# First attention: the next batch's normalization in four parts, its matmul pieces two a step, the rotary tables one part a step

## The chip, the core and the metric

The kernel runs on one core of one Trainium2 chip. The time is the device time of one launch in microseconds (us). Five instruction queues work side by side: TensorE (PE in the profile, its weight loads PEld), VectorE (DVE), ScalarE (ACT), GpSimd (POOL) and SyncE (SP), which here issues the DMAs. Each executes its own instructions in order; semaphores tie them together.

## The reference

All arrays are 32-bit floats; x is 8 batches of 512 tokens of 256 numbers. Four residual blocks follow each other:

```
x = x + attn_a(layernorm(x))     # 8 heads of 64, keys and values from a 64-wide latent
x = x + ffn(layernorm(x))        # 2 layers: local attention with rotary tables, then a gated MLP
x = x + attn_b(layernorm(x))     # 16 heads of 16, causal
x = x + ffn(layernorm(x))
```

What the change touches is the first block:

```
h = (x - mean(x)) / sqrt(var(x) + 1e-5)
q = h @ Wq.T ; lat = h @ Wkv_down.T
scores = q @ (lat @ Wk_up.T).T / 8 ; attn = softmax(scores)
x = x + concat(attn @ (lat @ Wv_up.T)) @ Wo.T
```

It also touches the preparation of the rotary tables, which the local attention of the second block multiplies its queries and keys with. These are cos and sin tables, scaled by position, times the learned query and key scales: two layers by four tables of 512 x 64 numbers.

## The kernel before

The eight batches go in two groups of four. Each group runs ten stages: the first attention (`attention_a`), two times local attention and feedforward, the second attention (`attention_b`), and again two times local attention and feedforward. A stage is a `head()`, whose parts the stage ahead calls one by one in its last steps, and a `run()`.

**Steps of the first attention.** A tile is 128 tokens. A unit is one pair of heads for one tile of queries (4 x 4 units a batch). Units go two at a time: `steps()` has 32 pairs in a group, so 8 steps a batch, numbered m = 0 to 31 (and two more to drain). In step m the scores of pair m are made, the probabilities of pair m-1 are transposed, and the values of pair m-2 are multiplied. On TensorE a step is: scores (4 matmuls, L393), values (16, L439), the transposes of one unit (8, L426), the transposes of the other unit, and in an odd step from m = 3 on the projection of a finished tile (4, L455). On VectorE: two maxima (L399), per unit the copy of its transposes out of PSUM (L430) and a reciprocal of its sums (L414), and in an odd step the add of the projection to x (L458). On ACT: in an odd step the copy of the values (oT, L449), then four exponentials (L244), then four divisions (L419). Everything issued in a step is tied, engine by engine, to the order in which the code writes it (`order_keeper`).

**Pieces.** The following batch's `prologue` is a generator that the steps advance: a piece in the middle of an odd step and one at the end of an even step. Its pieces are, in order: the layernorm (four times `bn_stats` and `bn_aggr` on VectorE, L279 and L280; two POOL operations for 1/sqrt, L269 and L270; four normalizing operations on VectorE, L286), two halves of the transposed yT (4 transposes each, copied by ACT, L352), pd (2 matmuls, copied to latT by VectorE, L359), pl (4 transposes, copied by ACT, L365) and four times pq (2 matmuls, copied to a part of qT by ACT, L376). The layernorm stands at the end of a batch's step 0, the last pq at the end of the next batch's step 0.

**Buffers.** PSUM: three buffers "s" of two banks, which scores and transposes take in turn (four a step); one bank "mm", which all pieces and the projection share; one bank "o" for the values. In SBUF the probabilities have three buffers "p".

**Tables.** `rotation_tables()` is called once, after the head of the first stage, in which step 0 of the first group is already issued. It loads the raw tables into a buffer "p", the scales into a buffer "two", and issues eight multiplications on VectorE (L230), outside the kept order. What is outside a kept order is placed by a scheduler when the program is built; so are the first parts of the next stage (for example the statistics `st_f0x` of the local attention), which stand where the scheduler puts them, between the instructions of a step.

**The second group's head.** Its parts are called two by two in the six rounds of the last feedforward batch of the group before, and two more times ahead of that batch's output matmuls. By then step 0 is issued.

Of the kernel before, what the change touches and what calls it, by code (L numbers as in the profile page):

```python
# [11 lines left out]
F32 = mybir.dt.float32  # L12
AF = mybir.ActivationFunctionType
ALU = mybir.AluOpType
# [3 lines left out]
P = 128  # L18
NB, T, D = 8, 512, 256
NT = T // P  # L20
GROUP = 4
H, HD = 8, 64
# [8 lines left out]
DEPTH = 2  # L31
EARLY_STEPS = 2
LN_EPS = 1e-5
# [16 lines left out]
def kernel(  # L50
# [26 lines left out]
    nc = tc.nc  # L77
# [5 lines left out]
    def load_x(b):  # L83
        xt = resid.tile([P, NT, D], F32, tag=f"x{b % GROUP}", name=f"x_{b}")
        nc.sync.dma_start(xt, x[b].rearrange("(t p) d -> p t d", p=P))
        return xt
# [7 lines left out]
    pool = ctx.enter_context(tc.tile_pool(name="work", bufs=2))  # L94
# [8 lines left out]
    xs = {0: load_x(0)}  # L103
# [115 lines left out]

    def rotation_tables():  # L220

        raw = pool.tile([P, 4, NT, HD], F32, tag="p", name="raw", bufs=3)
        nc.sync.dma_start(raw, rope.rearrange("c (t p) d -> p c t d", p=P))
        sc = pool.tile([P, DEPTH, 4, HD], F32, tag="two", name="sc", bufs=5)
        nc.sync.dma_start(
            sc.rearrange("p l c d -> p (l c d)"), f_scale.rearrange("l c d -> (l c d)").partition_broadcast(P)
        )
        for l in range(DEPTH):
            for c in range(4):
                nc.vector.tensor_mul(tabs[l][:, c], raw[:, c], sc[:, l, c].unsqueeze(1).to_broadcast([P, NT, HD]))  # L230

    tabs = [const.tile([P, 4, NT, HD], F32, name=f"tab{l}") for l in range(DEPTH)]

    phase = {"start": None, "last": [], "gates": False}
# [31 lines left out]
    def inv_sqrt(t, least, op, n, name):  # L266

        r = pool.tile([P, n], F32, tag=f"rs{n}", name=name, bufs=3)
        nc.gpsimd.tensor_scalar(r, t, least, 1.0, op, ALU.mult)  # L269
        nc.gpsimd.tensor_tensor(r, r, neg_half[:, :n], ALU.pow)  # L270
        return r

    def row_statistics(halves, name):

        st = pool.tile([P, NT, len(halves), 6], F32, tag=f"ln_st{len(halves)}", name=f"st_{name}", bufs=2)
        mv = pool.tile([P, NT, 2], F32, tag="ln_mv", name=f"mv_{name}", bufs=2)
        for t in range(NT):
            for i, h in enumerate(halves):
                nc.vector.bn_stats(st[:, t, i, :], h[:, t, :])  # L279
            nc.vector.bn_aggr(mv[:, t, :], st[:, t].rearrange("p i s -> p (i s)"))  # L280
        return mv, inv_sqrt(mv[:, :, 1], LN_EPS, ALU.add, NT, f"rstd_{name}")

    def normalize_rows(halves, dst, mv, rstd):
        for t in range(NT):
            for h, d in zip(halves, dst):
                nc.vector.tensor_scalar(  # L286
                    d[:, t, :], h[:, t, :], mv[:, t, 0:1], rstd[:, t : t + 1], ALU.subtract, ALU.mult
                )

    def layernorm(halves, dst, name):  # L290

        normalize_rows(halves, dst, *row_statistics(halves, name))

    def transposed(ps, rows, half, name):

        pt = ps.tile([P, NT, P], F32, tag="mm", name=name)
        for t in range(NT):
            nc.tensor.transpose(pt[:, t, :], rows[half][:, t, :], ident)
        return pt.rearrange("p t c -> p (t c)")

    def halves_of(rows):
        return [rows[:, :, 0:P], rows[:, :, P:D]]
# [7 lines left out]
    def attention_a(batches, g):  # L310
# [33 lines left out]
        def prologue(b):  # L344

            n = f"a{b}"
            yr = pool.tile([P, NT, D], F32, tag="yr", name=f"yr_{n}", bufs=1)
            layernorm([xs[b]], [yr], n)
            yield
            yT = pool.tile([P, 2, T], F32, tag="hT", name=f"yT_{n}")  # L350
            for k in range(2):
                nc.scalar.copy(yT[:, k, :], transposed(ps_mm, halves_of(yr), k, f"pyt_{n}_{k}"))  # L352
                yield

            pd = ps_mm.tile([P, T], F32, tag="mm", name=f"pd_{n}")
            for k in range(2):
                nc.tensor.matmul(pd, lhsT=wd_a[:, k, :], rhs=yT[:, k, :], start=(k == 0), stop=(k == 1))
            latT = pool.tile([P, T], F32, tag="two", name=f"latT_{n}", bufs=5)
            nc.vector.tensor_copy(latT, pd)  # L359
            yield  # L360
            pl = ps_mm.tile([P, NT, HD], F32, tag="mm", name=f"pl_{n}")
            for t in range(NT):
                nc.tensor.transpose(pl[:, t, :], latT[:HD, t * P : (t + 1) * P], ident[:HD, :HD])
            lat = pool.tile([P, NT, HD], F32, tag="lat", name=f"lat_{n}")
            nc.scalar.copy(lat, pl)  # L365
            yield
            qT = big([P, 4, T], f"qT_{n}")
            if b == batches[0]:
                fold()
            for m in range(4):  # L370
                pq = ps_mm.tile([P, T], F32, tag="mm", name=f"pq_{n}_{m}")
                for k in range(2):
                    nc.tensor.matmul(
                        pq, lhsT=wqk_a[:, k, m * P : (m + 1) * P], rhs=yT[:, k, :], start=(k == 0), stop=(k == 1)
                    )
                nc.scalar.copy(qT[:, m, :], pq)  # L376
                state[b] = qT, latT, lat
                yield
# [87 lines left out]
        each = NT * 2  # L466

        def steps(ahead):
            tables_of(EXP_TABLES)
            kept_order = order_keeper()  # L470
            pieces = iter(())

            def pair(m):
                return pairs[m] if 0 <= m < len(pairs) else ()

            for m in range(len(pairs) + 2):
                new, turning, weighted = pair(m), pair(m - 1), pair(m - 2)
                done = weighted[1] if weighted and m % 2 else None
                with kept_order():
                    for some in new:  # L480
                        some.scores()
                    for some in weighted:
                        some.values()
                    for some in new:
                        some.maxima()
                    if done:
                        done.keep_values()
                    for some in new:
                        some.exponentials()
                    if turning:  # L490
                        turning[0].turn()
                        turning[0].keep_turned()
                    if new:
                        new[0].invert()
                    if done:
                        next(pieces, None)
                    if new:
                        new[0].divide()
                    if turning:
                        turning[1].turn()  # L500
                        turning[1].keep_turned()
                    if new:
                        new[1].invert()
                        new[1].divide()
                    if done:
                        done.project()
                        done.add()
                    else:
                        next(pieces, None)
                    if m % each == 0 and m // each + 1 < len(batches):  # L510
                        pieces = prologue(batches[m // each + 1])
                        next(pieces)
                if m > len(pairs) - 3:
                    ahead[0]()
                    ahead[0]()
                yield

        follower = []
        rest = steps(follower)

        def head():
# [14 lines left out]
    def attention_f(batches, l, g, ys, first_layer):  # L536
# [287 lines left out]
        stats = {}  # L824
# [6 lines left out]
        def rows(at):  # L831
            b, t = tiles[at]
            if first_layer and t == 0:
                ys[b] = rows_space(b, f"y_{g}_{b}")
                normalize_rows([xs[b]], [ys[b]], *stats.pop(b))

        def begin(at):
            if tiles[at][1] == 0:
# [94 lines left out]
    def feedforward(batches, l, g, ys, last, finish, norms):  # L933
        w1, w2 = weights_g(l, g)

        h2s, stats, hns, hTs, made = {}, {}, {}, {}, {}
# [11 lines left out]
        def halves(b):  # L948
            return [ys[b][:, :, 0:P], h2s[b]]
# [4 lines left out]
        def rows(b):  # L954
            hn = pool.tile([P, 2, NT, P], F32, tag="yr", name=f"hn_g{g}_{b}", bufs=1)
            hns[b] = [hn[:, 0], hn[:, 1]]
            normalize_rows(halves(b), hns[b], *stats.pop(b))

        def columns(b, k):
            if k == 0:  # L960
# [135 lines left out]
    def normalized_b():  # L1096

        state, got = {}, {}

        def statistics(b):  # L1100
            got[b] = row_statistics([xs[b]], f"b{b}")

        def rows(b):
            yr = rows_space(b, f"yr_b{b}")
            normalize_rows([xs[b]], [yr], *got.pop(b))
            state[b] = {"yr": yr}

        return (statistics, rows), state
# [542 lines left out]
```

## Time and profile before

| | us |
|---|---|
| three runs | 4433.58, 4436.53, 4437.04 (median 4436.53) |
| the profiled execution | 4432.33 |
| its span, first to last instruction | 4430.5 |
| first attention, group 0, step 0 to step 31 | 27.2 to 293 |
| first attention, group 1, step 0 to step 31 | 2226.7 to 2489 |

The time of each step of the first attention is the distance between the starts of two steps' first score matmuls in the timeline (us):

| batch | 0 | 1 | 2 | 3 | 4 | 5 | 6 | 7 | sum |
|---|---|---|---|---|---|---|---|---|---|
| group 0, batch 0 | 6.90 | 14.17 | 6.22 | 9.34 | 6.23 | 9.66 | 7.43 | 9.66 | 69.61 |
| group 0, batch 1 | 7.43 | 11.32 | 6.22 | 9.34 | 6.23 | 9.66 | 7.43 | 9.66 | 67.29 |
| group 0, batch 2 | 7.43 | 13.68 | 6.22 | 9.34 | 6.22 | 9.66 | 7.43 | 9.66 | 69.64 |
| group 0, batch 3 | 7.43 | 9.79 | 6.23 | 8.67 | 6.22 | 8.67 | 6.22 | | |
| group 1, batch 0 | 12.01 | 5.40 | 6.23 | 9.33 | 6.23 | 9.66 | 7.43 | 9.66 | 65.94 |
| group 1, batch 1 | 7.43 | 11.33 | 6.22 | 9.34 | 6.22 | 9.66 | 7.43 | 9.66 | 67.30 |
| group 1, batch 2 | 7.43 | 13.18 | 6.22 | 9.33 | 6.23 | 9.66 | 7.43 | 9.66 | 69.14 |
| group 1, batch 3 | 7.43 | 9.79 | 6.22 | 8.67 | 6.22 | 8.67 | 6.22 | | |

In batch 3 there is no following batch, so from its step 1 on no pieces. Step 0 of group 1, batch 0, holds the output matmuls of the feedforward ahead. In the profile's rows, a bracket says how long the engine sat idle before the instruction and what ended that. Names are without buffer numbers: `s_a` scores, `nm_a` maxima, `p_a` probabilities, `ppt_a` and `pt_a` transposed probabilities in PSUM and SBUF, `o_a` values, `pp_a` projection, `rstd_a` the 1/sqrt of a normalization, `yr_a` its result; `f0x` and `f1x` are the local attention that follows in group 0 and 1. A matmul of these 32-bit numbers shows as two records.

### The profile page before, as it was taken

How to read it: one execution, taken by the hardware profiler on the slowest of the kernel's cores; microseconds unless marked ns; L12 is line 12 of the kernel's file. 1: busy time of each engine (PE TensorE's matmuls, PEld its weight loads, DVE VectorE, ACT ScalarE, POOL GpSimd, SP SyncE). 2: the span in 40 equal slices, each digit the busy share in tenths (PEclk: the TensorE clock that was granted, in tenths of full speed). 3: DMA queues.
4: the chain of work that ended last, by engine and by line, in shares of the span. 5: the costliest groups of instructions: out<-in, count | busy, mean ns of one | idle time of the engine just before them, and what ended most of it. 6: DMA issues, size and time to landing. Idle time of an engine off the chain costs nothing.

```text
span 4430.5 us, 70536 instructions
## 1 busy us (share of the span) xinstructions
PE 4175.9 (94%) x26580; PEld 2547.3 (57%) x26580; DVE 3073.0 (69%) x7497; ACT 2690.1 (61%) x6316; POOL 1147.7 (26%) x1140
## 2 busy tenths in 40 slices
PE   8999999999998899999999999999999988999999
PEld 5656556654555465566566565565545554655655
DVE  5668737846999887377466686377379998863773
ACT  5767616716989675177166675276178986742761
POOL 0014313311222342143100242143122223422431
PEclk9999999999999999999999999999999999999999
DMA  2000000000000000000100000000000000000000
GB/s 82 1 22 4 21 6 23 4 24 20 1 1 1 20 4 7 3 23 13 53 30 1 20 4 23 22 3 22 6 21 2 1 1 20 4 6 22 3 4 23
DMA packets 51091, 63.36 MB, mean 14 GB/s; under 512 B 6336, under 2 KB 45504, under 8 KB 50752
## 3 DMA queue, kind: packets, MB, share of 16 engines
q1 hardware_dynamic: 50752, 58.85, 4.1%
q8 instruction: 211, 3.46, 0.3%
q14 instruction: 128, 1.05, 0.1%
HBM read 46.28 MB, written 4.19 MB: 11 GB/s over the span
## 4 chain that ended last, share of the span: by engine, by line
PE 72%; DVE 14%; ACT 12%; issue 1%; POOL 1%; DMA 0%; SPq 0%; POOLq 0%; ACTq 0%; DVEq 0%
PE pu_g1x L983 3%; PE pu_g0x L983 3%; PE pu_g0y L983 3%; PE pu_g1y L983 3%; PE o_a L439 3%; PE s_a L393 3%; PE pqk_f0y L561 2%; PE pqk_f1y L561 2%; PE pqk_f0x L561 2%; PE pqk_f1x L561 2%; ACT r_b L244 2%; PE ppt_a L426 2%; PE ppt_b L1320 2%; DVE pt_b L1325 2%; ACT num_b L244 2%; DVE r_b L1271 2%
## 5 line engine op out<-in xcount | busy, mean ns | idle before, releaser
L1320 PE MATMUL ppt_b<-ident,num_b 128*128 128x128 f32 x1280 | 223.3, 291 | 89.5 <-DVE pt_b L1325 64.3
L1320 PEld LDWEIGHTS ppt_b<-ident,num_b 128*128 128x128 f32 x1280 | 137.4, 143 | 274.0 <-ACT num_b L244 96.7
L244 ACT ACTIVATE num_b<-num_b,most_b 128x512 f32<-128x512 f32 (+3 forms) x512 | 280.7, 552 | 20.2 <-POOL most_b L1300 19.8
L1325 DVE COPY pt_b<-ppt_b 128x512 f32<-128x512 f32 (+1 forms) x352 | 223.7, 635 | 31.7 <-PE ppt_b L1320 30.9
L244 ACT ACTIVATE p_a<-s_a,nm_a 128x512 f32<-128x512 f32 x256 | 173.3, 688 | 102.3 <-DVE nm_a L399 70.4
L430 DVE COPY pt_a<-ppt_a 128x1024 f32<-128x1024 f32 x128 | 155.7, 1219 | 106.3 <-PE ppt_a L426 106.3
L1267 DVE TENSOR_TENSOR t_b<-den_b,r_b 128x1024 f32<-128x1024 f32 (+1 forms) x176 | 197.1, 1120 | 45.5 <-ACT r_b L244 45.0
L1290 DVE CUSTOM_DVE_ANT_0 num_b<-num_b,r_b 128x512 f32<-128x512 f32 (+3 forms) x512 | 223.6, 485 | 1.2 <-POOL num_b L1283 1.2
L1283 POOL TENSOR_TENSOR num_b<-num_b,causal 128x256 f32<-128x256 f32 (+2 forms) x176 | 173.7, 987 | 184.1 <-ACT num_b L1277 183.6
L1248 PE MATMUL den_b<-st_b,st_b 18*128 18x384 f32 (+3 forms) x1024 | 208.0, 472 | 0.4 <-ACT num_b L1277 0.4
L1271 DVE SCALAR_TENSOR_TENSOR r_b<-t_b,r_b 128x1024 f32<-128x1024 f32 (+1 forms) x176 | 204.5, 1162 | 0.2
L1248 PE MATMUL dot_b<-st_b,st_b 16*128 16x384 f32 (+3 forms) x1024 | 189.5, 471 | 5.8 <-ACT yT_b L1126 4.4
L244 ACT ACTIVATE p_f0y<-p_f0y,nm_f0y,rn_f0y 128x256 f32<-128x256 f32 (+1 forms) x256 | 143.8, 563 | 80.6 <-DVE nm_f0y L700 80.5
L244 ACT ACTIVATE p_f1y<-p_f1y,nm_f1y,rn_f1y 128x256 f32<-128x256 f32 (+1 forms) x256 | 143.8, 564 | 80.6 <-DVE nm_f1y L700 80.5
L244 ACT ACTIVATE p_f1x<-p_f1x,nm_f1x,rn_f1x 128x256 f32<-128x256 f32 (+1 forms) x256 | 143.8, 564 | 76.8 <-DVE nm_f1x L700 76.7
L244 ACT ACTIVATE p_f0x<-p_f0x,nm_f0x,rn_f0x 128x256 f32<-128x256 f32 (+1 forms) x256 | 143.7, 563 | 76.8 <-DVE nm_f0x L700 76.8
L244 ACT ACTIVATE r_b<-den_b 128x1024 f32<-128x1024 f32 (+1 forms) x176 | 165.8, 942 | 36.6 <-PE dot_b L1248 17.7
L1300 POOL TENSOR_SCALAR most_b<-most_b 128x2 f32<-128x2 f32 (+2 forms) x176 | 34.2, 194 | 568.7 <-DVE most_b L1290 553.4
L1277 ACT ACTIVATE num_b<-dot_b 128x1024 f32<-128x1024 f32 (+1 forms) x176 | 164.6, 935 | 27.7 <-PE dot_b L1248 27.6
L399 DVE TENSOR_REDUCE nm_a<-s_a 128x2 f32<-128x1024 f32 x128 | 151.0, 1219 | 37.1 <-PE s_a L393 37.1
L244 ACT ACTIVATE r_b<-r_b 128x1024 f32<-128x1024 f32 (+1 forms) x176 | 172.5, 980 | 5.6
L603 POOL TENSOR_TENSOR ro_f1x<-ro_f1x,rs_f1x 128x512 f32<-128x512 f32 x64 | 80.4, 1278 | 363.0 <-DVE rs_f1x L592 149.7
(356 smaller groups left out, 11279.7 us busy)
## 6 DMA issues: line engine op xcount, KB each, us to landing
x<-in_x SPq DMA_DIRECT2D x8, 512.0 KB
out<-x SPq DMA_DIRECT2D x8, 512.0 KB
wf_0x<-in_f_wqkv SPq DMA_DIRECT2D x2, 1536.0 KB
wf_0y<-in_f_wqkv SPq DMA_DIRECT2D x2, 1536.0 KB
wf_1x<-in_f_wqkv SPq DMA_DIRECT2D x2, 1536.0 KB
wf_1y<-in_f_wqkv SPq DMA_DIRECT2D x2, 1536.0 KB
wg_0x<-in_f_w SPq DMA_DIRECT2D x2, 1386.0 KB
wg_0y<-in_f_w SPq DMA_DIRECT2D x2, 1386.0 KB
```

The source lines that it names most:

```text
L244: i = nc.scalar.activation(out, in_, func, **more).ins
L430: nc.vector.tensor_copy(got["pt"], got.pop("ppt"))
L561: nc.tensor.matmul(dst.rearrange("p h d -> p (h d)"), lhsT=hTs[b][:, k, t * P : (t + 1) * P], rhs=wqkv[:, k, c * INNER : (c + 1) * INNER], ...
L983: nc.tensor.matmul(pu[: cols.stop - cols.start, c], lhsT=w1[:, k, cols], rhs=hT[:, k, :], start=(k == 0), stop=(k == 1),)
L1248: return nc.tensor.matmul(s[:, a, m * width : (m + 1) * width], lhsT=left[at, j, past:width], rhs=right[at, j, :width], start=True, stop=True,
L1267: nc.vector.tensor_mul(t[:, :, :cols], den[:, :, :cols], r[:, :, :cols])
L1271: nc.vector.scalar_tensor_tensor(r[:, :, :cols], t[:, :, :cols], 2.0, r[:, :, :cols], ALU.subtract, ALU.mult)
L1277: nc.scalar.activation(num[:, :, :cols], dot[:, :, :cols], AF.Square, scale=-0.5)
L1283: nc.gpsimd.tensor_add(own, own, mask)
L1290: nc.vector.tensor_tensor_reduce(out=s4[:, a, m, :], in0=s4[:, a, m, :], in1=r4[:, a, m, :], scale=-1.0, scalar=LOWEST, op0=ALU.mult, op1= ...
L1320: nc.tensor.transpose(ppt[:, k, :], p[:, a, k * P : (k + 1) * P], ident)
L1325: nc.vector.tensor_copy(pt[:, a, :nblocks, :], ppt[:, :nblocks, :])
```

## The change

- The layernorm piece becomes four pieces: statistics of two tiles, statistics of the other two and the POOL operations, normalization of two tiles, normalization of the other two. The twelve pieces of a batch are advanced once at the end of every step, and once more in the middle of steps 4 to 7. So steps 0 to 3 carry one part of the normalization each, and steps 4 to 7 two pieces with matmuls each, the second after the projection and its add. No piece is left for the next batch's step 0.
- The raw tables go to the buffers "rs" and "ro", which only the local attention uses, and the eight multiplications are issued one a step in steps 4 to 11 of the first group, in kept order after the piece.
- The second group's head has three calls more and so fills all twelve calls of the six rounds.
- `row_statistics` and `normalize_rows` take a range of tiles and return or take one value more; their other callers do what they did.

```diff
     def rotation_tables():
-        raw = pool.tile([P, 4, NT, HD], F32, tag="p", name="raw", bufs=3)
+        raw = pool.tile([P, 4, NT, HD], F32, tag="rs", name="raw", bufs=1)
         nc.sync.dma_start(raw, rope.rearrange("c (t p) d -> p c t d", p=P))
-        sc = pool.tile([P, DEPTH, 4, HD], F32, tag="two", name="sc", bufs=5)
+        sc = pool.tile([P, DEPTH, 4, HD], F32, tag="ro", name="sc", bufs=3)
...
-        for l in range(DEPTH):
-            for c in range(4):
-                nc.vector.tensor_mul(tabs[l][:, c], raw[:, c], sc[:, l, c].unsqueeze(1).to_broadcast([P, NT, HD]))
+        def table(l, c):
+            nc.vector.tensor_mul(tabs[l][:, c], raw[:, c], sc[:, l, c].unsqueeze(1).to_broadcast([P, NT, HD]))
+        later.extend(lambda l=l, c=c: table(l, c) for l in range(DEPTH) for c in range(4))
...
-    def row_statistics(halves, name):
+    def row_statistics(halves, name, tokens=range(NT), made=None):
-        st = pool.tile([P, NT, len(halves), 6], F32, tag=f"ln_st{len(halves)}", name=f"st_{name}", bufs=2)
-        mv = pool.tile([P, NT, 2], F32, tag="ln_mv", name=f"mv_{name}", bufs=2)
-        for t in range(NT):
+        if made:
+            st, mv, _ = made
+        else:
+            st = pool.tile([P, NT, len(halves), 6], F32, tag=f"ln_st{len(halves)}", name=f"st_{name}", bufs=2)
+            mv = pool.tile([P, NT, 2], F32, tag="ln_mv", name=f"mv_{name}", bufs=2)
+        for t in tokens:
...
-        return mv, inv_sqrt(mv[:, :, 1], LN_EPS, ALU.add, NT, f"rstd_{name}")
+        rstd = inv_sqrt(mv[:, :, 1], LN_EPS, ALU.add, NT, f"rstd_{name}") if tokens[-1] == NT - 1 else None
+        return st, mv, rstd
...
         def prologue(b):
             n = f"a{b}"
+            some = None
+            for tokens in (range(2), range(2, NT)):
+                some = row_statistics([xs[b]], n, tokens, some)
+                yield
             yr = pool.tile([P, NT, D], F32, tag="yr", name=f"yr_{n}", bufs=1)
-            layernorm([xs[b]], [yr], n)
-            yield
+            for tokens in (range(2), range(2, NT)):
+                normalize_rows([xs[b]], [yr], *some[1:], tokens)
+                yield
...
-                    if done:
+                    if m % each > 3:
                         next(pieces, None)
...
                     if done:
                         done.project()
                         done.add()
-                    else:
-                        next(pieces, None)
                     if m % each == 0 and m // each + 1 < len(batches):
                         pieces = prologue(batches[m // each + 1])
-                        next(pieces)
+                    next(pieces, None)
+                    if later and m > 3:
+                        later.popleft()()
```

More of the change, by code (lines that the diff above doesn't have):

```diff
@@ L227, in rotation_tables @@
         )
-        for l in range(DEPTH):
-            for c in range(4):
-                nc.vector.tensor_mul(tabs[l][:, c], raw[:, c], sc[:, l, c].unsqueeze(1).to_broadcast([P, NT, HD]))
+        def table(l, c):
+            nc.vector.tensor_mul(tabs[l][:, c], raw[:, c], sc[:, l, c].unsqueeze(1).to_broadcast([P, NT, HD]))
+        later.extend(lambda l=l, c=c: table(l, c) for l in range(DEPTH) for c in range(4))
+    later = deque()
     tabs = [const.tile([P, 4, NT, HD], F32, name=f"tab{l}") for l in range(DEPTH)]
@@ L280, in row_statistics, with normalize_rows @@
             nc.vector.bn_aggr(mv[:, t, :], st[:, t].rearrange("p i s -> p (i s)"))
-        return mv, inv_sqrt(mv[:, :, 1], LN_EPS, ALU.add, NT, f"rstd_{name}")
-    def normalize_rows(halves, dst, mv, rstd):
-        for t in range(NT):
+        rstd = inv_sqrt(mv[:, :, 1], LN_EPS, ALU.add, NT, f"rstd_{name}") if tokens[-1] == NT - 1 else None
+        return st, mv, rstd
+    def normalize_rows(halves, dst, mv, rstd, tokens=range(NT)):
+        for t in tokens:
             for h, d in zip(halves, dst):
@@ L290, in layernorm @@
     def layernorm(halves, dst, name):
-        normalize_rows(halves, dst, *row_statistics(halves, name))
+        normalize_rows(halves, dst, *row_statistics(halves, name)[1:])
     def transposed(ps, rows, half, name):
@@ L834, in rows @@
                 ys[b] = rows_space(b, f"y_{g}_{b}")
-                normalize_rows([xs[b]], [ys[b]], *stats.pop(b))
+                normalize_rows([xs[b]], [ys[b]], *stats.pop(b)[1:])
         def begin(at):
@@ L956, in rows @@
             hns[b] = [hn[:, 0], hn[:, 1]]
-            normalize_rows(halves(b), hns[b], *stats.pop(b))
+            normalize_rows(halves(b), hns[b], *stats.pop(b)[1:])
         def columns(b, k):
@@ L1104, in rows @@
             yr = rows_space(b, f"yr_b{b}")
-            normalize_rows([xs[b]], [yr], *got.pop(b))
+            normalize_rows([xs[b]], [yr], *got.pop(b)[1:])
             state[b] = {"yr": yr}
```

## The prediction

> **What bounds the kernel now.** I read the page's busy shares and chain first, then the timeline of the two first-attention stretches (27 to 290 us, 2227 to 2489 us), because the order of instructions shows that only these stretches and the end of the stage ahead of the second one change.
>
> ```profile
> span 4430.5 us, 70536 instructions
> ...
> PE 4175.9 (94%) x26580; PEld 2547.3 (57%) x26580; DVE 3073.0 (69%) x7497; ACT 2690.1 (61%) x6316; POOL 1147.7 (26%) x1140
> ...
> PE 72%; DVE 14%; ACT 12%; issue 1%; POOL 1%; DMA 0%; SPq 0%; POOLq 0%; ACTq 0%; DVEq 0%
> ```
>
> TensorE carries the chain, and its work is the same in both kernels. So only its waits count, and the change can only trade one wait for another.
>
> The wait that the change attacks, in step 9 (batch 1, step 1; start, duration, operation, idle before it):
>
> ```profile
> 107.81 1.38 DVE L286 TENSOR_SCALAR yr_a<-x,mv_a,rstd_a 128x256 f32<-128x256 f32 x4 [1.41 <-POOL rstd_a L270]
> ...
> 111.87 1.09 PE L426 MATMUL ppt_a<-ident,p_a 128*128 128x128 f32 x8 [1.12 <-ACT p_a L244]
> ...
> 113.68 1.99 PE L455 MATMUL pp_a<-wa,oT_a 128*128 128x256 f32 x8 [0.72 <-ACT yT_a L352]
> ```
>
> VectorE holds the maxima back for GpSimd, but TensorE pays only 1.12+0.72 us for it, and 0.85 at 106.26 for a late qT copy. In step 1 it pays far more (first line below). The last batch, here steps 26 and 27 on TensorE alone, shows steps that have no piece at all, and the add after a projection:
>
> ```profile
> 44.92 1.97 PE L426 MATMUL ppt_a<-ident,p_a 128*128 128x128 f32 x8 [5.94 <-ACT p_a L244]
> ...
> 254.82 1.97 PE L426 MATMUL ppt_a<-ident,p_a 128*128 128x128 f32 x16
> 257.23 1.99 PE L393 MATMUL s_a<-latT_a,qT_a 64*128 64x512 f32 x8 [0.44 <-DVE pt_a L430]
> 259.15 1.97 PE L439 MATMUL o_a<-pt_a,lat_a 128*64 128x128 f32 x32
> 261.05 1.09 PE L426 MATMUL ppt_a<-ident,p_a 128*128 128x128 f32 x8
> 263.15 1.09 PE L426 MATMUL ppt_a<-ident,p_a 128*128 128x128 f32 x8 [1.01 <-ACT p_a L244]
> ...
> 266.01 0.42 DVE L458 TENSOR_TENSOR x<-pp_a,x 128x256 f32<-128x256 f32 x1 [0.43 <-PE pp_a L455]
> ```
>
> The second unit's exponentials start only when the first transposes have freed a p buffer (at 256.00, 1.18 after those began, ACT idle for 1.11), and the next scores need the PSUM buffer that these exponentials free; in the odd step the exponentials stand behind ACT's copy of oT. So a step without a piece waits anyway: 6.22 us for 5.62 of work (even), 8.67 for 7.54 (odd). A piece laid there costs less than its own time.
>
> **The change part by part.** Steps 0 to 7 are a batch's own (m modulo 8); higher numbers count through the group. TensorE blocks from start to start: scores 1.92, values 1.90, a unit's transposes 0.90, projection 1.92; pieces: yT half 0.61, pd or pq 1.82, pl 0.42.
>
> *Normalization in parts.* A statistics part is 1.07 us of VectorE (104.20 to 105.27), a normalizing part 0.7 (half of 1.38). After an even step it lies ahead of the odd step's maxima; these end at +3.5 us, while ACT first copies oT (to +4.4) and the transposes that VectorE copies next end at +4.95: about 1.4 us of cover. After an odd step, 0.64 of idle and 0.8 of slack at the second transposes cover it. POOL's 1.3 us now lie a whole step before their reader. Cost 0, with at most 1.07 per batch if the cover fails. A table part (2.76/8 = 0.35) fits into the same cover.
>
> *Steps 0 to 3 without pieces:* 6.22+8.67+6.22+8.67 = 29.78. Batch 1 now: 7.43+11.32+6.22+9.34 = 34.31. Gain 4.53.
>
> *Step 4, two yT halves* through the one "mm" buffer: the second waits until ACT has done two exponentials and the first copy: 1.18+1.34+0.57+0.05 = 3.14 after the first transposes start, where TensorE is there at 0.90+0.61+0.90 = 2.41. Wait 0.73: 3.82+3.14+0.61 = 7.57 for 6.23.
>
> *Step 5, pd and pl:* pl needs "mm" after the projection, thus the add, which starts 0.11 after it and takes 0.42 (266.01): wait 0.58. 9.34+0.58+0.42 = 10.34 for 9.66.
>
> *Step 6, two pq:* the first copy is done at 3.40, the second pq due at 3.62: no wait, 5.62+3.64 = 9.26 for 7.43.
>
> *Step 7, two pq:* 9.66+0.58+1.82 = 12.06 for 9.66.
>
> Steps 4 to 7: 39.23 against 32.98, loss 6.25. A middle batch gets 69.01 for 67.29: **+1.7**.
>
> *Batch 1* in both groups: +1.7 each. *Batch 3:* step 24 loses its leftover pq (7.43 to 6.22), step 25 its wait for qT (9.79 to 8.67): −2.3 each.
>
> *Batch 0, group 0.* The tables' 2.76 us and raw's p buffer leave step 1. By the rows, the exponentials then follow the maxima at 39.50 and 40.84, and step 3 starts near 49.85 instead of 54.53: −4.7. This counts 1.2 us of half clock, which the 1.7 us wait at 37.7 still brings. Steps 3 to 7: −0.67+1.34+0.68+1.83+2.40 = +5.6. Sum **+0.9** (−0.3 with full clock).
>
> *Batch 0, group 1.* The old normalization cost nothing: it ran under the output matmuls of the stage ahead (2232 to 2237 us). Nothing is gained in step 1 but 0.2. The same steps 3 to 7 add 5.6: **+5.4**. In that head the pieces move later by three calls of 13; one pq now lies between two score matmuls, which then no longer run side by side: 3×0.96 for 1.92, **+1.0**.
>
> *Batch 2.* The next attention's statistics are hoisted into it, and in the new order its normalization stands between step 18's two maxima. It waits for POOL, where that power stands behind this batch's:
>
> ```profile
> 175.02 0.20 POOL L269 TENSOR_SCALAR rstd_f0x<-mv_f0x 128x4 f32<-128x4 f32 x1
> 175.29 1.01 POOL L270 TENSOR_TENSOR rstd_a<-rstd_a,neg_half 128x4 f32<-128x4 f32 x1
> 176.27 1.16 POOL L270 TENSOR_TENSOR rstd_f0x<-rstd_f0x,neg_half 128x4 f32<-128x4 f32 x1
> ...
> 180.39 1.34 PE L426 MATMUL ppt_a<-ident,p_a 128*128 128x128 f32 x8 [2.28 <-ACT p_a L244]
> ```
>
> From the statistics' end to the second power's end is 2.8 us, of which the first maximum hides 1.2. VectorE then normalizes two tiles (0.66) before the second maximum. Laid out from step 17's start: hoisted statistics 1.5+1.6+0.3, the step's own 1.2, so step 18's maxima stand at 11.3 and 14.8, its second exponentials at 16.0, the next scores at 17.45 instead of 14.89: +2.56. So 69.01+2.56 = 71.57 against 69.64 (group 0) and 69.14 (group 1): +1.9 and +2.4. TensorE idles 2.55 us at once. What that does to the clock, step 17 shows (a row of the table by windows: window, length, then busy time and count of PE, PEld, DVE, ACT and POOL, granted clock, DMA):
>
> ```profile
> 171.00:186.00 15.00, 11.40 (x74) 7.33 (x74) 12.58 (x38) 8.79 (x19) 2.54 (x5) 0.89 0.00 1
> ```
>
> After 2.28 us of idle the mean clock is 0.89, that is half clock for some 3.4 us, and the step cost 1.45 us more than step 9's shape and the added idle explain (13.68−11.32−0.91); after 1.12 us, in step 9, the mean stayed 1.00. Between 0 and 1.45 each; I take 0.9, as a wait may straddle two such stretches: **+2.8 and +3.3**.
>
> [...]
>
> *DMAs.* The raw tables' load (512 KB) stands some five issues earlier on SP, ahead of the next weights, which are due over 200 us later: 0.
>
> Sum: group 0 0.9+1.7+2.8−2.3 = 3.1; group 1 1.0+5.4+1.7+3.3−2.3 = 9.1; together **+12.2 us** on 4432.3 (span 4430.5 and 1.8 around it), 0.28%. That execution lies 4.2 us under the median of 4436.5, so I forecast 4448.7.
>
> **Rivals.** *The double pieces are cheaper:* if the add and the copies answer faster than the rows here (no wait of 0.73 and 0.58 twice: −1.89 in six batches, −11.3), the kernel gains little or loses little: +1, 4437.5. For it: the projection's own wait for such a copy was only 0.23. Against: the add follows the projection by dependency.
>
> *Not slower:* steps without pieces lose their waits, these being a habit of the last batch. Place: steps 0 to 3; price 2×(0.60+1.13) = 3.46 in six batches, 20.8: 12.2−20.8 = −8.6, 4428. It decides from 2.0 us a batch on. Against: steps 26 to 30 repeat to 0.01 us in both groups, and buffers cause the wait.
>
> *VectorE's parts show:* the cover fails by 1.07 in each of two odd steps per batch, 12.8 more: +25, 4461. For it: table and statistics together are 1.42, just the cover.
>
> **How the numbers follow.** Forecast 0.65, cheap pieces 0.17, not slower 0.08, VectorE shows 0.10. About 0.2% (8.9 us) is what can be told from no change. The forecast's unknowns (clock 0 to 2.9 us in batch 2 and 1.2 in step 1) leave 0.05 of it under that line; the not-slower case splits evenly. Slower 0.65−0.05+0.10 = 0.70, same 0.05+0.17+0.04 = 0.26, faster 0.04. The range 4437 to 4459 runs from the cheap pieces to just short of the last rival; the not-slower case and that rival's tail stay out.
>
> **What would show it.** Right: steps 1 and 3 of a batch near 8.67, step 7 near 12; pl and every fourth pq waiting about 0.58 for the add of L458's successor; in steps 18 a VectorE wait for rstd_f0x and rstd_f1x and about 2.5 us of idle TensorE. Wrong: odd steps without pieces at 7.6, or maxima that the exponentials wait for in odd steps.

## The result

The changed kernel takes 4444.36 us (median of 19 runs, 4441.19 to 4450.81) against 4434.62 us (median of 19, 4431.10 to 4438.83). The ratio is 1.0022 with a 95% interval of 1.0015 to 1.0029: 6.7 to 12.9 us slower (9.7 between the medians), where 12.2 was forecast. The profiled execution of the changed kernel took 4445.76 us, and its span is 13.4 us longer than that of before.

From the page of the changed kernel, busy time and chain:

```profile
span 4443.9 us, 70535 instructions
...
PE 4182.0 (94%) x26580; PEld 2549.5 (57%) x26580; DVE 3073.9 (69%) x7497; ACT 2693.1 (61%) x6316; POOL 1147.2 (26%) x1140
...
PE 72%; DVE 14%; ACT 12%; issue 1%; POOL 1%; DMA 0%; SPq 0%; POOLq 0%; ACTq 0%; DVEq 0%
```

The work and the shares of the chain are those of before. What has moved is where TensorE waits, and for that the steps have to be read. The table gives the distance from one step's first score matmul to the next, in us, from the timelines (before / after):

| batch | 0 | 1 | 2 | 3 | 4 | 5 | 6 | 7 | sum |
|---|---|---|---|---|---|---|---|---|---|
| group 0, batch 0, before | 6.90 | 14.17 | 6.22 | 9.34 | 6.23 | 9.66 | 7.43 | 9.66 | 69.61 |
| after | 6.90 | 7.92 | 7.81 | 8.67 | 7.56 | 10.10 | 9.28 | 12.16 | 70.40 |
| group 0, batch 1, before | 7.43 | 11.32 | 6.22 | 9.34 | 6.23 | 9.66 | 7.43 | 9.66 | 67.29 |
| after | 6.22 | 8.67 | 6.22 | 8.67 | 7.56 | 10.10 | 9.28 | 12.16 | 68.90 |
| group 0, batch 2, before | 7.43 | 13.68 | 6.22 | 9.34 | 6.22 | 9.66 | 7.43 | 9.66 | 69.64 |
| after | 6.22 | 8.67 | 9.07 | 8.67 | 7.56 | 10.10 | 9.28 | 12.16 | 71.75 |
| group 1, batch 2, before | 7.43 | 13.18 | 6.22 | 9.33 | 6.23 | 9.66 | 7.43 | 9.66 | 69.14 |
| after | 6.23 | 8.67 | 9.07 | 11.44 | 7.56 | 10.10 | 9.28 | 12.16 | 74.52 |

TensorE in step 9 (batch 1, step 1) of the changed kernel, from the timeline: start, duration, operation, idle before it.

```profile
104.77 1.97 PE L451 MATMUL o_a<-pt_a,lat_a 128*64 128x128 f32 x32
106.67 1.09 PE L438 MATMUL ppt_a<-ident,p_a 128*128 128x128 f32 x8
108.78 1.09 PE L438 MATMUL ppt_a<-ident,p_a 128*128 128x128 f32 x8 [1.01 <-ACT p_a L247]
109.71 1.89 PE L467 MATMUL pp_a<-wa,oT_a 128*128 128x256 f32 x8
111.53 1.99 PE L405 MATMUL s_a<-latT_a,qT_a 64*128 64x512 f32 x8
```

VectorE's 1.41 us of waiting for GpSimd is gone from this step, but the 1.01 us that an odd step waits for its own exponentials is still there, now with no piece to fill it. The pieces went to steps 4 to 7, and there they wait for each other. The end of step 7, on TensorE:

```profile
161.10 1.99 PE L467 MATMUL pp_a<-wa,oT_a 128*128 128x256 f32 x8 [0.23 <-ACT qT_a L388]
163.62 1.98 PE L385 MATMUL pq_a<-yT_a,wa 128*128 128x512 f32 x4 [0.52 <-DVE x L470]
```

The projection waits for the copy of the first pq, and the second pq for the projection's add: the one "mm" bank is handed on three times in a row.

Step 18 (batch 2, step 2), first on GpSimd and then on VectorE:

```profile
183.39 1.01 POOL L273 TENSOR_TENSOR rstd_a<-rstd_a,neg_half 128x4 f32<-128x4 f32 x1
184.36 1.01 POOL L273 TENSOR_TENSOR rstd_f0x<-rstd_f0x,neg_half 128x4 f32<-128x4 f32 x1
```

```profile
182.67 1.19 DVE L411 TENSOR_REDUCE nm_a<-s_a 128x2 f32<-128x1024 f32 x1
185.40 0.74 DVE L293 TENSOR_SCALAR y_0x<-x,mv_f0x,rstd_f0x 128x256 f32<-128x256 f32 x2 [1.54 <-POOL rstd_f0x L273]
186.05 1.22 DVE L411 TENSOR_REDUCE nm_a<-s_a 128x2 f32<-128x1024 f32 x1
```

The second maximum stands behind a normalization that waits for the second of two powers. What TensorE makes of it, in group 0 and in group 1 (timeline, then the table by windows with the granted clock as the third number from the end):

```profile
189.50 1.99 PE L405 MATMUL s_a<-latT_a,qT_a 64*128 64x512 f32 x8 [3.01 <-DVE pt_a L442]
...
2400.55 3.78 PE L405 MATMUL s_a<-latT_a,qT_a 64*128 64x512 f32 x8 [3.01 <-DVE pt_a L442]
2404.26 2.94 PE L451 MATMUL o_a<-pt_a,lat_a 128*64 128x128 f32 x32
```

```profile
2396.00:2410.00 14.00, 9.91 (x67) 6.51 (x66) 9.64 (x19) 7.15 (x18) 1.68 (x4) 0.76 0.00 0
185.00:199.00 14.00, 9.92 (x80) 6.99 (x79) 11.48 (x24) 9.93 (x23) 1.62 (x4) 1.00 0.00 1
```

The same wait of 3.01 us costs no clock in group 0 (granted clock 1.00); in group 1 (0.76) the next scores take 3.78 us for 1.99 and step 19 grows from 8.67 to 11.44.

The 13.4 us of the two profiles add up like this. To the first exponential of the local attention, group 0 is 1.2 later (318.61, now 319.80). From a fixed instruction of the feedforward ahead of group 1's first attention (an operation of ACT on the MLP's gate, shortly before the head's first part) to the same point in group 1 it is 378.41, now 389.62: +11.2. The two second attentions, which nothing in the change touches, give +7.4 and -6.0; all else -0.4. That the second attentions differ is the clock: their windows show it, of before and then of after.

```profile
1069.00:1528.00 459.00, 406.58 (x3737) 227.81 (x3729) 418.64 (x921) 393.53 (x778) 110.77 (x187) 0.99 0.01 1
3270.00:3735.00 465.00, 414.76 (x3705) 232.13 (x3706) 417.52 (x919) 391.67 (x778) 110.30 (x185) 0.97 0.02 6
```

```profile
1070.00:1537.00 467.00, 417.68 (x3741) 234.26 (x3734) 419.41 (x924) 393.65 (x779) 111.25 (x187) 0.96 0.01 1
3290.00:3749.00 459.00, 407.61 (x3706) 227.73 (x3706) 417.39 (x923) 391.45 (x777) 109.69 (x184) 0.99 0.02 6
```

From the stage's first value product to its last it takes 454.7 us in both stretches with a mean clock of 0.99, and 460.7 and 462.1 where it is 0.97 and 0.96. Single executions of one kernel scatter by 5 to 14 us within a set of runs, so in the experiments the steps of the first attention are read, and a single whole time is not. From step 3 of a group on, and where no half clock falls into them, these repeat to 0.02 us from group to group.

### The profile page after: what moved, and what is told of

It is laid out like the page before. It is cut to its first block, busy times and chain, and to the rows that moved or that the text cites. A ratio compares the mean times of both kernels' runs of the same rounds, so it can differ in the third digit from the quotient of the medians.

```text
span 4443.9 us, 70535 instructions
## 1 busy us (share of the span) xinstructions
PE 4182.0 (94%) x26580; PEld 2549.5 (57%) x26580; DVE 3073.9 (69%) x7497; ACT 2693.1 (61%) x6316; POOL 1147.2 (26%) x1140
## 4 chain that ended last, share of the span: by engine, by line
PE 72%; DVE 14%; ACT 12%; issue 1%; POOL 1%; DMA 0%; SPq 0%; POOLq 0%; ACTq 0%; DVEq 0%
PE pu_g0y L995 3%; PE pu_g0x L995 3%; PE pu_g1x L995 3%; PE pu_g1y L995 3%; PE s_a L405 3%; PE o_a L451 3%; PE pqk_f0y L573 2%; PE pqk_f1y L573 2%; ACT r_b L247 2%; PE pqk_f1x L573 2%; PE pqk_f0x L573 2%; PE ppt_a L438 2%; PE ppt_b L1332 2%; DVE pt_b L1337 2%; ACT num_b L247 2%; DVE r_b L1283 2%
```

## The experiments

**The tables alone.** The kernel before, with the new `rotation_tables()` and one table part a step:

```diff
                         pieces = prologue(batches[m // each + 1])
                         next(pieces)
+                    if later and m > 3:
+                        later.popleft()()
```

> The kernel before with only the rotary tables changed (other buffers, one part a step from step 4 on). Theory: the 2.76 us of table parts between the two maxima of step 1 and the p buffer that the raw tables held were the part of group 0's step 1 that no other batch has, so step 1 falls from 14.17 us to between 9.5 and 11.4 (step 9, which has the same whole normalization, takes 11.32), the rest of batch 0 stays within 0.1 us a step, and the table parts in steps 4 to 11 cost nothing. Rival: VectorE has no room for 0.35 us a step; then steps 4 to 11 each grow by up to 0.35, 2.8 in all. Whole kernel 3 to 5 us under the kernel before by the theory, 0 to 2 by the rival. Nothing in group 1 changes by either.

Step 1 of group 0 fell only to 13.46 us, and step 2 rose from 6.22 to 6.66: 0.3 us for both, not 3 to 5. The whole normalization in front of the maxima sets this step, with or without the tables: TensorE idles 5.85 us there (5.94 before). Seven of the eight table parts cost nothing. One shows what such a part can do: issued at the end of step 8, it stands ahead of step 9's maxima and behind the normalization that waits 1.41 us for GpSimd. TensorE in step 9:

```profile
110.58 1.09 PE L429 MATMUL ppt_a<-ident,p_a 128*128 128x128 f32 x8 [1.46 <-ACT p_a L247]
112.39 3.48 PE L458 MATMUL pp_a<-wa,oT_a 128*128 128x256 f32 x8 [0.72 <-ACT yT_a L355]
```

TensorE's wait is 1.46 us in place of 1.12, the projection takes 3.48 us for 1.99, as at half clock, and the step takes 13.15 for 11.32. One run took 4428.15 us, beside 4429.91 for one of the kernel before: too close to tell.

**The four parts undone.** The changed kernel with the normalization in one piece at the end of step 0:

```diff
-            for tokens in (range(2), range(2, NT)):
-                some = row_statistics([xs[b]], n, tokens, some)
-                yield
             yr = pool.tile([P, NT, D], F32, tag="yr", name=f"yr_{n}", bufs=1)
-            for tokens in (range(2), range(2, NT)):
-                normalize_rows([xs[b]], [yr], *some[1:], tokens)
-                yield
+            layernorm([xs[b]], [yr], n)
+            yield
...
-                    next(pieces, None)
+                    if m % each not in (1, 2, 3):
+                        next(pieces, None)
```

> The changed kernel, but with the normalization in one piece at the end of a batch's step 0, as before; the pieces with matmuls stay two a step in steps 4 to 7. Theory: the whole piece holds VectorE back for GpSimd, so step 1 of a middle batch takes 10.4 to 10.8 us (11.32 before, less the 0.61 of the piece it had) against 8.67 with four parts; step 17 takes 12.5 to 13.3; steps 18 fall from 9.07 to 6.22, since this batch's power is long done when the next attention's normalization asks for GpSimd. Steps 4 to 7 as in the changed kernel (7.56, 10.10, 9.28, 12.16). So the four parts are worth about 2 us a batch, and in batch 2 some 1.5 more or less. Rival: the step without a piece hides the normalization as the table parts are hidden; then step 1 takes 8.67 to 9.2 and the four parts are worth nothing.

Steps 18 came out at 6.23 in both groups and steps 4 to 7 as in the changed kernel, as the theory had it: the wait in step 18 is made by the new order. But step 1 took 13.56 and 13.10 us, not 10.4 to 10.8, and step 17 took 14.74 and 14.59. Without the piece that stood between its two waits, TensorE idles in one stretch:

```profile
112.34 1.09 PE L433 MATMUL ppt_a<-ident,p_a 128*128 128x128 f32 x8
117.65 1.81 PE L433 MATMUL ppt_a<-ident,p_a 128*128 128x128 f32 x8 [4.22 <-ACT p_a L247]
```

and half clock follows (the projection takes 2.90 us for 1.99; the mean granted clock from 108 to 126 us is 0.91). So with the pieces out of step 1 the four parts are worth 4.4 to 4.9 us in batch 1, the half clock included, over twice what was expected; in batch 2 the longer step 18 takes part of it back. The time was 4459.9 us in one run. This version's head has as many calls as that of before, and the stretch from that gate to step 2 of group 1 takes 108.16 us (before 108.60, changed kernel 109.70): the three added calls of the head cost 1.5 us.

**The normalization one step earlier** for batches 2 and 3:

```diff
-                    if m % each == 0 and m // each + 1 < len(batches):
-                        pieces = prologue(batches[m // each + 1])
-                    next(pieces, None)
+                    if m == 0:
+                        pieces = prologue(batches[1])
+                    if m < each or m % each != 3:
+                        next(pieces, None)
+                    if m % each == each - 1 and m // each + 2 < len(batches):
+                        pieces = prologue(batches[m // each + 2])
+                        next(pieces)
```

> The changed kernel, but for batches 2 and 3 of a group the four parts of the normalization stand one step earlier (steps 7, 0, 1, 2 in place of 0, 1, 2, 3); batch 1's stay. Theory: the 3.01 us wait of step 18 is GpSimd's queue (the next attention's power behind this batch's) and VectorE's order; with this batch's power a step earlier, the next attention's normalization is ready 1.0 us sooner and 1.1 us of statistics leave VectorE's way, so step 18 falls from 9.07 us to 6.2 to 6.8 in both groups, and step 19 of group 1 from 11.44 to 8.67, since the wait that brought the lower clock is gone. Rival: it is the next attention's own two normalizing operations and their power ahead of the second maximum; then step 18 stays at 8 or above. All other steps as in the changed kernel, within 0.1; whole kernel 5 to 8 us below the changed one by the theory, under 3 by the rival.

Most numbers hold (step 18 at 6.39 and 6.40, step 19 of group 1 at 8.67, 4437.24 us in one run), but step 17 was to stay at 8.67 and takes 8.95, and the reason given is not the one at work. The scheduler moved the next attention's statistics along, so the two powers still follow each other, now in step 17:

```profile
174.12 1.19 DVE L411 TENSOR_REDUCE nm_a<-s_a 128x2 f32<-128x1024 f32 x1
176.85 0.41 DVE L293 TENSOR_SCALAR y_0x<-x,mv_f0x,rstd_f0x 128x256 f32<-128x256 f32 x1 [1.54 <-POOL rstd_f0x L273]
177.18 1.22 DVE L411 TENSOR_REDUCE nm_a<-s_a 128x2 f32<-128x1024 f32 x1
```

VectorE waits the same 1.54 us. Step 17 is 0.28 us longer with it, step 18 was 2.84 longer. By the rows, ACT copies oT ahead of its exponentials in an odd step, and they are late anyway (TensorE waits 1.01 us for them here as in step 9 of the changed kernel); also, one normalizing operation stands ahead of the second maximum here, and two did in step 18. So the run shows that the wait's place matters, and says nothing on GpSimd's queue.

**One power less.** That needed another run:

```diff
-        nc.gpsimd.tensor_tensor(r, r, neg_half[:, :n], ALU.pow)
+        if name not in ("rstd_a3", "rstd_a7"):
+            nc.gpsimd.tensor_tensor(r, r, neg_half[:, :n], ALU.pow)
```

> The changed kernel without GpSimd's power in the normalization of the last batch of each group (that batch's rows are then scaled by the variance itself, which leaves out 1.0 us of GpSimd and alters the numbers only). Theory: VectorE's wait of 1.54 us in step 18 holds 1.0 us of queue behind this power; it falls to 0.5 and step 18 from 9.07 to 8.0 to 8.2 us in both groups. Rival: the wait is for the next attention's own statistics and power; then step 18 stays within 0.2 of 9.07. Nothing else changes by more than the clock's chance.

Step 18 takes 8.08 us in both groups. VectorE in step 18 of this run:

```profile
184.49 1.19 DVE L412 TENSOR_REDUCE nm_a<-s_a 128x2 f32<-128x1024 f32 x1
186.24 0.74 DVE L294 TENSOR_SCALAR y_0x<-x,mv_f0x,rstd_f0x 128x256 f32<-128x256 f32 x2 [0.55 <-POOL rstd_f0x L274]
186.89 1.22 DVE L412 TENSOR_REDUCE nm_a<-s_a 128x2 f32<-128x1024 f32 x1
```

0.55 for 1.54, and 0.99 of the step with it. GpSimd's queue is 1.0 us of the 2.84. No run takes the rest apart; the rows have 0.55 us of waiting for the next attention's own power and 0.65 of normalizing ahead of the second maximum.

**The projection in a bank of its own.** The changed kernel, one line:

```diff
-                got["pp"] = pp = ps_mm.tile([P, D], F32, tag="mm", name=f"pp_{n}")
+                got["pp"] = pp = ps_o.tile([P, D], F32, tag="o", name=f"pp_{n}")
```

> The changed kernel with the projection in the PSUM bank of the values (o) in place of the one that the pieces use (mm). Theory: the second piece of steps 5 and 7 waits only for the projection's add (0.52 us idle in both), and the projection of step 7 for a copy of qT (0.23); both go. Step 5 falls from 10.10 us to 9.4 to 9.6, step 7 from 12.16 to 11.3 to 11.5, together 1.2 to 1.5 us a batch, in six batches 7 to 9 us. Steps 4 and 6 stay at 7.56 and 9.28. Rival: the next scores wait anyway, for the copy of the transposes that frees their buffer, as in the steps without a piece; then steps 5 and 7 fall by under 0.3 us. In batch 3 the pieces of the next attention may move, since the bank is free more often: there no step should grow.

One run took 4422.43 us. Step 5 fell from 10.10 to 9.34 us and step 7 from 12.16 to 10.88, together 2.04 a batch, more than expected; steps 4 and 6 stayed. The end of step 7 (from the timed run of the same kernel, below) has no wait left:

```profile
159.60 1.89 PE L467 MATMUL pp_a<-wa,oT_a 128*128 128x256 f32 x8
161.33 1.88 PE L385 MATMUL pq_a<-yT_a,wa 128*128 128x512 f32 x4
163.14 1.99 PE L405 MATMUL s_a<-latT_a,qT_a 64*128 64x512 f32 x8
```

One expectation failed: in batch 3, where matmuls of the next attention now move into the waits, two steps grew from 6.22 to 6.57. What they took along left the start of the next stage: from step 31 to that stage's first exponential it is 27.8 us for 31.6.

**The same line in the kernel before.**

> The kernel before with only the projection moved to the o bank. Theory: the waits of the projection for the copy of a piece go (0.72 us in step 1, about 0.23 in steps 3, 5 and 7), some 1.4 us a batch in six batches, and in batch 3 the free bank lets the next attention's transposes and value products into the steps' waits, as the run with the bank showed, some 3 us a group: 12 to 15 us in all, 4417 to 4423. Rival: only the doubled pieces needed the bank; then under 3 us.

One run took 4408.19 us. Step 1 fell from 11.32 to 10.33, step 3 from 9.34 to 9.16, steps 5 and 7 from 9.66 to 9.16: a batch of 65.13 us for 67.29. In batch 3 the next attention's transposes and value products stand in the waits:

```profile
251.28 0.60 PE L298 MATMUL pht_f0x<-ident,y_0x 128*128 128x128 f32 x4
...
256.63 1.88 PE L561 MATMUL pv_f0x<-wf_0x,hT_f0x 128*128 128x512 f32 x4
```

This was more than the theory had, so both kernels with the bank were timed side by side.

> The kernel before with the projection in the o bank, timed against the kernel before. Its single run stood at 4408, of which its steps explain 19 us and the second attention's clock the rest; theory: the bank alone is worth 17 to 22 us, ratio 0.995 to 0.9962. Rival: the single run was a lucky one; then under 12 us.

> The changed kernel with the projection in the o bank, timed against the kernel before. Theory: the change's other costs (two pq in one step, the head of group 1, GpSimd's queue in step 18) do not depend on the bank; by steps it then lies 6 to 14 us above the kernel before with the bank, 4421 to 4428, ratio 0.996 to 0.9985. Rival: the shared bank was all that made the change lose; then it lies level with the kernel before with the bank.

The kernel before with the bank: 4406.82 us, ratio to the kernel before 0.9941 (0.9927 to 0.9955), 20 to 32 us; the 27 between the medians are more than the 17 to 22 expected. The changed kernel with the bank: 4423.45 us, ratio 0.9973 (0.9963 to 0.9983). The change costs 16.6 us between these two medians, more than the 6 to 14 expected: the bank helps both kernels, and the one before more. By the profile, the bank's gain in the kernel before is 8 us up to the start of group 0's local attention, 9 in group 1, 2 in the feedforward blocks and 5 in the second attentions. How much of that last part is the clock's chance, and so how much of the 27 us between the medians is the bank's, stays open.

**A version from these runs.** The normalization moves a whole batch ahead, into steps 4 to 7 where its reader is a batch away; the pieces go one a step from step 0 on.

```diff
-                    if m % each > 3:
+                    if m % 2:
                         next(pieces, None)
...
-                    next(pieces, None)
+                    if not m % 2:
+                        next(pieces, None)
+                    if m % each == 4 and m // each + 2 < len(batches):
+                        parts = normalization(batches[m // each + 2])
+                    if m % each > 3:
+                        next(parts, None)
```

Here `normalization(b)` is the four parts cut from `prologue(b)`. The first batch's is done in one go in the head, the second's four parts beside the head's four pq. It was run with the projection in the o bank and without.

> A version made from the runs so far. The normalization's four parts stand in steps 4 to 7 of the batch before the one that needed them until now (batch 1's beside the first batch's q matmuls), so yr is ready at a batch's step 0; the pieces with matmuls then go one a step (end of even, middle of odd steps) over steps 0 to 7, with no leftover; table parts one a step; the projection has the o bank. Theory (a piece laid into a step with a wait costs less than its own time, a second one costs all of it): a middle batch takes 6.22, 8.67 to 8.9, 7.43, 8.67 to 9.0, 7.43, 9.4, 7.43, 9.4, together 64.6 to 65.2 us, against 67.29 before, 68.90 in the changed kernel and 66.85 with the bank alone; step 18 pays at most 1 us for the next attention's normalization. Against the kernel before: batch 0 of group 0 -3 to -5, batches 1 -2.3 each, batches 2 -4 each, batches 3 -2 each, the start of the attention that follows -3 each: 4409 to 4414 us, ratio 0.995. Rival: with yr's parts ahead of a batch's maxima in steps 4 to 7 VectorE becomes the limit (odd steps with a part above 10.1); then no better than the bank alone, 4420.

> The same without the change of bank. Theory: the projection and the pieces share one bank, and with one piece a step only the projection waits, 0.23 us for a copy: odd steps with a piece take 9.1 to 9.66, and a middle batch 65.4 to 66. Nothing of the next attention moves into batch 3, whose steps are 6.22 and 8.67. So 4420 to 4425 us. Rival: the bank matters as much as with two pieces a step; then a middle batch takes 66.9 or more.

With the bank: 4399.79 us (4394.76 to 4405.76), ratio to the kernel before 0.9921 (0.9907 to 0.9934), below the 4409 to 4414 expected. This interval overlaps that of the bank alone (0.9927 to 0.9955), so the gain over the bank alone rests on the steps. Batch 2 takes 6.23, 8.67, 7.43, 8.67, 7.43, 9.16, 7.43, 9.16, in sum 64.18; batch 1 takes 65.16, since the next attention's statistics now fall into its steps 13 and 14, where the wait of 1.54 us for the second power costs 0.98. The start of group 1 got dearer: from the gate to its step 2 it is 111.42 us, for 108.60 before. The profiled execution took 4394.76 us at a mean granted clock of 0.995, that of before 4432.33 at 0.992. Without the bank it took 4415.12 in one run, under the 4420 to 4425 expected, but of the steps the rival's number came true: 66.94 for batch 2. TensorE in step 9 without the bank, and with it:

```profile
105.36 1.09 PE L446 MATMUL ppt_a<-ident,p_a 128*128 128x128 f32 x8 [0.58 <-ACT p_a L247]
107.17 1.99 PE L475 MATMUL pp_a<-wa,oT_a 128*128 128x256 f32 x8 [0.72 <-ACT yT_a L372]
```

```profile
103.24 1.09 PE L446 MATMUL ppt_a<-ident,p_a 128*128 128x128 f32 x8 [0.57 <-ACT p_a L247]
104.17 1.89 PE L475 MATMUL pp_a<-wa,oT_a 128*128 128x256 f32 x8
```

One piece a step is enough to make the projection wait for the shared bank. The bank is worth 2.76 us a batch here, against 2.04 with the pieces in pairs.

## Why the prediction was right

The time lies in the range and the way is the one forecast; the medians lie 9.7 us apart, where 12.2 was forecast. Of the 4.3 us between 4448.7 and 4444.36, 1.9 come from the base (4436.53 as the median of three runs, 4434.62 of 19). Term by term, as the change against the kernel before (us):

| step of the prediction | forecast | in the profile |
|---|---|---|
| steps 0 to 3 without pieces, middle batch | -4.53 | -4.53 |
| step 4 / 5 / 6 / 7 | 7.57 / 10.34 / 9.26 / 12.06 | 7.56 / 10.10 / 9.28 / 12.16 |
| batch 0, group 0 | +0.9 | +0.8 |
| batch 0, group 1, with its head | +6.4 | +6.6 |
| batch 1, each | +1.7 | +1.6 |
| batch 2, group 0 / group 1 | +2.8 / +3.3 | +2.1 / +5.4 |
| batch 3, each | -2.3 | -2.3 |
| start of the first step, group 0 | 0 | -1.0 |

Batch 0 of group 1 is taken from the gate named above to the start of batch 1. The sum was 12.2 and is 12.4 in this pair of executions; that it fits so closely is luck, as the three terms below show. The -1.0 is no gain of the change: the first step starts at 26.23 us in the changed kernel, at 27.56 in the run with the whole normalization, and at 26.56 and 27.06 in two executions of one kernel.

The central step, that a step without a piece waits anyway, so that a piece laid there is cheap and a second one dear, was read off the last batch: its 6.22 and 8.67 us came out to 0.01 us, and the doubled pieces to 0.24 us or better. With one piece a step, in the last version without the bank, a middle batch takes 66.94 us for 68.90. Why such a step waits (the p buffers, and the order on ACT) was read off the rows; no run gave it another buffer. The other side came out too: "Not slower" asked for steps 0 to 3 without waits, and they keep them. "VectorE's parts show" is out as well: the odd steps stand at 8.67. Of "cheaper double pieces" only 0.24 in step 5 came true: the next scores start at 144.09 us, before pl ends at 144.37.

Three terms were off in their size or their cause, and the sum hides it.

*The clock in step 18.* I bounded it by 0 to 1.45 us a group and took 0.9 for each. It was 0 in group 0 and 2.77 in group 1. The upper bound came from step 17, where the granted clock was 0.50 for 3.41 us (181.09 to 184.50 in the profile of before); here it was 0.50 for 6.83 us (2399.47 to 2406.30 in that of the changed kernel). The 0.9 between the bounds was my choice; no run shows the reason given for it, a wait that straddles two stretches. The 1.45 was too much even for step 17: in group 1 of the run with the tables alone that step takes 12.56, so my estimate for half clock is 1.12 of its 13.68. The stall itself was 2.84, forecast 2.56: the transposes also took 2.24 us for 1.97.

*Batch 0 of group 0.* The -4.7 in steps 1 and 2 came out as -4.66, but I put it on the tables and on the buffer that the raw tables held, with the normalization. The run with the tables alone shows 0.3 for these; with the tables moved and the normalization whole, steps 1 and 2 take 20.07 us together, with its four parts 15.73 (there with the granted clock at 0.50 from 40.86 to 44.27 us), so nearly all of it is the normalization's. Part of the close fit is chance: in the run with one power less, which changes nothing there, the same two steps gained 3.8.

*The head of group 1.* One pq between two score matmuls was set at +1.0 and step 1 at -0.2. Measured against the run with the shorter head it is 1.5, with -0.4 for step 1.

What the split itself is worth was not in the prediction: had the normalization stayed whole, the emptied step 1 of batch 1 would have cost 4.4 to 4.9 us more.

The prediction asked only what the change does to the waits for one bank. That the bank was worth more than the move of the pieces, as the runs with it show, stood in the profile of before: 0.72 us ahead of the projection in step 9, and batch 3's waits with nothing to fill them.

## What to carry to other kernels

Before moving pieces of work between the steps of a loop, find a step of the profile that has none, and subtract its work from its length: that is what a piece can hide, once per step (here 6.22 less 5.62 us in an even step, which takes 7.43 with a pq of 1.82). Pieces in pairs hand their buffer on in sequence and pay for every copy between (0.23 and 0.52 us in step 7); one piece a step, and a second buffer, come first. Follow every wait to its queue and its place: steps with the same 1.54 us wait for GpSimd came out 0.28, 0.98 and 2.84 us longer, by where it stood and what stood beside it.

## What was not expected of the hardware

A wait of one length was followed by a lower clock in one place and not in another. In the first attentions of the profiles of before and of the changed kernel, from a group's step 3 on, TensorE has two waits of over 2 us each. In that of before they are 2.28 and 2.29 us, in step 17 of both groups, and the granted clock is 0.50 from 181.09 to 184.50 us and from 2375.86 to 2379.27. In that of the changed kernel they are 3.01 us, in step 18 of both groups: in group 0 the clock stays at 1.00 from 185 to 199 us, in group 1 it is 0.50 from 2399.47 to 2406.30. These stretches do not all begin behind the wait: in group 0 of before 0.70 us after its end, in group 1 0.30 us ahead of its end, in group 1 of the changed kernel 1.08 us ahead of it.

Two steps of the other runs belong here. In the run with one power less, the scores behind a wait of 2.02 us in step 18 take their 1.99 us; in the run with the tables alone, the projection behind waits of 1.46 and 0.72 us takes 3.48 us for 1.99. And in a second attention of the changed kernel the clock is 0.50 from 1419.84 to 1423.25 us, with TensorE busy for 2.71 of the 3.41 us just ahead. So in these cases the length of a wait does not tell whether the clock falls. What does is not shown: no run moved a wait with all else kept.
